# A graph network on one core: node features put in graph order by two scatters, indexed moves spaced out, and layer 0's edge weight as a polynomial on GpSimd

## The chip, the cores and the metric

The kernel runs on one core of one Trainium2 chip. A core has five engines that each work through their own list of instructions: TensorE (PE, with its weight loads shown apart as PEld), VectorE (DVE), ScalarE (ACT), GpSimd (POOL) and SyncE (SP), which here only issues DMAs. They meet at semaphores. The metric is the time of the program on the device in microseconds; lower is better.

## What is computed

There are 128 graphs of 64 nodes with 128 features each (`x`), and a 64x64 matrix `adj` for every graph, in which about a quarter of the entries are above zero (in a symmetric pattern). Four layers follow one another, each with a residual and a layernorm: `x = layernorm(x + layer(x, adj))`. The first two are message passings over the edges, and nearly all of the time is theirs:

```python
# layer 0: distance d = adj[i, j]
f_ij = jnp.exp(coeff * diff * diff)                 # 20 Gaussians of d
rcut = 0.5 * (jnp.cos(d_ij * (math.pi / CUTOFF)) + 1.0) * (d_ij < CUTOFF)
W = ssp(f_ij @ fw1 + fb1) @ fw2 + fb2               # ssp(x) = softplus(x) - log 2
agg = jnp.einsum('bjf,bijf->bif', y, W * rcut[..., None])   # y = x @ w_in2f
out = ssp(agg @ ow1 + ob1) @ ow2 + ob2
...
# layer 1: the same form with 64 Gaussians, and the entry of adj itself, twice, as the weight
```

Layers 2 and 3 are graph convolutions with a normalised `adj`. The part that the change touches is `rcut`, which depends on the distance alone: 0.5(cos(πd/5) + 1) is the square of cos(πd/10), and 0 from d = 5 on.

## The kernel before, in words

**Only edges that are there are computed.** The kernel (`sparse_stack`) sorts the graphs by their number of edges, and the nodes of each graph by their degree. Two graphs make a pair, so that their 2 x 64 nodes fill the 128 partitions. There are 64 pairs, in 8 sets `s` of 8 pairs (`part(s)`), and all pairs of a set have the same number of edge slots per node. `graph_to` (L891) is the new place of each graph; an indexed scatter (L892) writes all of `adj` in that order to the HBM scratch `adj_sorted`, from which `load_a` reads a set's matrices into `a_all`. The features are not sorted: `load_x(s)` (L1288) fetches each pair's 128 rows of `x` from the input by an indexed gather into `x_all[:, p, :]` (L1291), 8 per set, with the indices `at_row` that `find_rows` makes. Set 0 is different: its graphs are the first 16 as they stand, and a plain DMA loads them.

**Building the edge lists.** For a set `s`, `permuted(s)` (L1022) moves the rows of its matrices into the order of degrees: 8 indexed scatters of `a_all` rows to `perm` in HBM (helper `scatter`, L1017), then 16 SP loads back into the tile `ad` (L1057). `nearest(s)` (L1129) then finds each row's entries in descending order on DVE, eight at a time: MAX8 (L1155), FIND_INDEX8 (L1158), and two instructions that knock out what was found (L1163, L1167). `pack(0, s, ...)` (L1066) puts distances, indices and weights of the edges into slots: `dc` (distance minus 5, at least −5; the `tensor_scalar` with `max` at L1083) and `jc` (indices, L1097) on POOL, and the weight `w`, which is cos(πd/10) by a Sin on ACT, with a bias of π/2 (L1102), squared on POOL (DVE for set 0; L1104). The three go to HBM (`store`), and the main loop reads them back slot by slot (L1265). After `pack`, `edges` (DVE, L1175) counts what was found and writes to the first half of the tile `same`, which the search has used as its scratch; `equal` (POOL, L1178; DVE, L1183) uses the second half. At last `spread(s)` (L1194) sends the found rows by 8 indexed scatters to `rows1[s]`, from which layer 1's slots are packed.

**The function `act`.** All ACT work goes through `act` (L927). Exp, Ln, Square and Copy are in one table set, Sin is in another. `act` puts a table load ahead of each Sin and one after it (L935) and ties the order.

**The order of the work.** The main loop (L1874) has 128 slots (64 pairs for each of the two layers) of 3 chunks. A chunk is: `filter_in` (PE L1731, then Exp and Ln on ACT), `filter_out` (PE L1744), `gather` (PE L1757 with the one-hot matrix `hot`, then a copy on ACT), `message` (DVE L1772) and `slot_sums` (DVE L1796, L1800). `hot` is built once a slot on DVE from `j` and `w` (L1716). All other work is cut into steps by generators, and the loop takes some steps of each at every chunk: `run(early, ...)` takes 9, later 2 or 5, steps of `gathering`, which runs `compact(s)` for sets 1 to 7 one after the other; `run(side, 1)` takes one step of `spread`. Within `compact(s)`, `spread_out` (L1111) takes one step of the moves for the next set (`permuted(s + 1)`, then `load_x(s + 1)`) at every `PACE`-th (4th) step of the search, and what is left of them at the end. Set 0's edges are built before the loop. The order in which the steps are written out is the order on each engine: `in_order` fixes it for DVE and POOL before the loop and for all five engines inside it. So an instruction that has to wait holds up all that stands behind it on its engine. `edges`, for instance, stands on DVE ahead of the messages of later chunks.

Of the kernel before, what the change touches and what calls it, by code (L numbers as in the profile page):

```python
# [69 lines left out]
ROUNDS = (5, 4, 4, 4, 4, 3, 3, 3)  # L70
FAR = -1e30
X_LIMIT = 40.0


def offsets1():
# [526 lines left out]
def sparse_stack(ctx: ExitStack, tc: tile.TileContext, t: dict, out: bass.AP, flag):  # L602
# [59 lines left out]
    nc.vector.memset(ones, 1.0)  # L662
    neg_half = const.tile([P, NP], F32, name="neg_half")
    nc.gpsimd.memset(neg_half, -0.5)
    half_pi = const.tile([P, 1], F32, name="half_pi")
    nc.vector.memset(half_pi, PI / 2)
    half = const.tile([P, 1], F32, name="half")
    nc.vector.memset(half, 0.5)
    one = const.tile([P, 1], F32, name="one")
# [21 lines left out]
    a_all = const.tile([P, NP, A + 1], F32, name="a_all")  # L691

    adj_sorted = dram.tile([NB, A, A], F32, name="adj_sorted")
    x_all = const.tile([P, NP, C], F32, name="x_all")
    x_pairs = x.rearrange("(p b) n c -> (b n) p c", b=2)
    x_rows, out_rows = (v.rearrange("g n c -> (g n) c") for v in (x, out))

# [87 lines left out]
    def wait_steps(n):  # L785
        yield from (None for _ in range(n))
# [73 lines left out]
    with (  # L860
        tc.tile_pool(name="count", bufs=2) as pre,
        tc.tile_pool(name="count_ps", bufs=1, space=PSUM) as ps_pre,
    ):
        entries = pre.tile([NB, A, A], F32, name="entries", bufs=1)
        some = pre.tile([NB, A, A], BF16, name="some", bufs=1)
        within = pre.tile([NB, A, A], BF16, name="within", bufs=1)
        for q in range(4):
            cut = slice(16 * q, 16 * (q + 1))
            nc.sync.dma_start(entries[:, cut, :], adj[:, cut, :])
            nc.vector.tensor_scalar(within[:, cut, :], entries[:, cut, :], CUTOFF, None, ALU.is_lt)  # L870
            nc.vector.tensor_scalar(some[:, cut, :], entries[:, cut, :], 0.0, None, ALU.is_gt)


        degree, close = given[:, 0, :], given[:, 1, :]
        run(deque([count(some, pre, degree), count(within, pre, close)]), -1)
        nc.vector.scalar_tensor_tensor(close, close, -float(A), degree, ALU.add, ALU.add)

        total = const.tile([NB, 1], F32, name="total")
        nc.vector.tensor_reduce(total, given[:, 0:2, :], AX.XY, ALU.add)
        nc.vector.tensor_scalar(total, total, key_of[:, 0:1], key_of[:, 1:2], ALU.mult, ALU.add)  # L880
        keys = pre.tile([P, P], F32, name="keys", bufs=1)
        nc.vector.tensor_scalar(keys, ident, total, None, ALU.mult)
        keys_ps = ps_pre.tile([P, P], F32, name="keys_ps")
# [37 lines left out]

    fence, latest, kind = None, None, None

    def act(out_, in_, func, **kw):  # L927
        nonlocal fence, latest, kind
        now = func == AF.Sin
        if kind is None or now != kind:  # L930
            fence = latest
            if not now:
                ctx_ = tc.issue_after(fence.ins) if fence is not None else nullcontext()
                with ctx_:
                    fence = nc.scalar.preload_act_table_set("natural_log_exp_and_others")  # L935
            kind = now
        with tc.issue_after(fence.ins) if fence is not None else nullcontext():
            latest = nc.scalar.activation(out_, in_, func, **kw)  # L938
        return latest

# [125 lines left out]
    def pack(layer, s, d, j):  # L1066

        caps, bases = CAPS[layer][s], BASES[layer][s]
        even, odds = EVEN[layer][s], ODD[layer][s]

        def packed(name, dt):
            tile_ = cpt.tile([P, max(EVEN[layer])], dt, tag=f"{name}{layer}", name=f"{name}{layer}_{s}")
            return tile_[:, 0:even]

        dc, jc = packed("dc", F32), packed("jc", BF16)
        for r in range(8):
            to = slice(bases[r], bases[r] + caps[r])  # L1080
            engine = nc.vector if layer + s == 0 and r % 2 else nc.gpsimd
            if layer == 0:
                engine.tensor_scalar(dc[:, to], d[:, r, 0 : caps[r]], -CUTOFF, None, ALU.max)  # L1083
            else:
                engine.tensor_copy(dc[:, to], d[:, r, 0 : caps[r]])
            if r % 2:
                yield

        def store(name, tile_):
            for h, size in enumerate((even, odds)):  # L1090
                to = dram_ap(slots[layer, name][s], h * even, [[even + odds, 64], [1, size]])
                nc.sync.dma_start(to, tile_[64 * h : 64 * (h + 1), 0:size])

        store("d", dc)
        for r in range(8):
            to = slice(bases[r], bases[r] + caps[r])
            nc.gpsimd.tensor_copy(jc[:, to], j[:, r, 0 : caps[r]])  # L1097
        store("j", jc)
        w = packed("w", F32)
        if layer == 0:  # L1100
            yield from wait_steps(6 if s else 0)
            act(w, dc, AF.Sin, bias=half_pi, scale=PI / (2 * CUTOFF))  # L1102
            yield from wait_steps(PACE if s else 0)
            (nc.gpsimd if s else nc.vector).tensor_tensor(w, w, w, ALU.mult)  # L1104
        else:
            nc.gpsimd.tensor_tensor(w, dc, dc, ALU.mult)
        store("w", w)
        stored.add((layer, s))
        yield

    def spread_out(work, ahead, every):  # L1111

        for n, _ in enumerate(work):
            if n % every == 0:
                next(ahead, None)
            yield
        yield from ahead

    def compact(s):


        ahead = iter(())
        if 0 < s < NS - 1:
            ahead = chain(permuted(s + 1), load_x(s + 1))
        if 0 < s < NS - 2:
            load_a(s + 2)
        yield from spread_out(nearest(s), ahead, PACE)

    def nearest(s):  # L1129

# [20 lines left out]
        for k in range(max(ROUNDS)):  # L1151
# [9 lines left out]
            if more:  # L1161
# [4 lines left out]
                yield  # L1166
                nc.vector.scalar_tensor_tensor(now, gone[:, 0:more], FAR, now, ALU.mult, ALU.add)  # L1167
                yield
        yield from pack(0, s, top, at)


        edges, equal = (
# [21 lines left out]
    def spread(s, comb):  # L1194

        for r in range(8):
            scatter(
                rows1[s].rearrange("q a k -> q (a k)"),
                comb[:, r, :, :].rearrange("p a k -> p (a k)"), goes[s][:, r : r + 1],
            )  # L1200
            yield
        rows = big(f"rows{s}").rearrange("p (r a k) -> p r a k", r=8, a=2)
        nc.sync.dma_start(rows, rows1[s].rearrange("(q r) a k -> q r a k", r=8))
        yield
        yield
        yield from pack(1, s, rows[:, :, 0, :], rows[:, :, 1, :])
# [80 lines left out]

    def load_x(s):  # L1288

        for p in range(8 * s, 8 * (s + 1)):  # L1290
            nc.gpsimd.indirect_dma_start(  # L1291
                out=x_all[:, p, :], out_offset=None, in_=x_rows,
                in_offset=bass.IndirectOffsetOnAxis(ap=at_row[:, p : p + 1], axis=0),
            )
            yield

    load_a(0)
    nc.sync.dma_start(x_all[:, part(0), :], x_pairs[:, part(0), :])
# [138 lines left out]
    nc.tensor.matmul(u[:, 0:1], lhsT=w["w2"], rhs=h0, start=True, stop=True)  # L1437

    run(deque([node_before(0, 0)]), -1)
    run(deque([compact(0)]), -1)  # L1440
    zero_filter = const.tile([P, 1], F32, name="zero_filter")
    nc.vector.tensor_add(zero_filter, u[:, 0:1], w["b2"])
# [391 lines left out]
    slot_data[0] = loads(0, nc.scalar)  # L1834
    slot_data[1] = loads(1)
    run(deque([permuted(1)]), -1)
    side.append(load_x(1))
    nc.sync.dma_start(caps_dram, caps_row.rearrange("o s i r -> o (s i r)"))
    nc.sync.dma_start(
        caps.rearrange("g i r -> g (i r)"), dram_ap(caps_dram, 0, [[18, NS], [0, 16], [1, 18]])  # L1840
# [33 lines left out]
    for i in range(3 * N + 2):  # L1874
# [3 lines left out]

        run(sums, (1, 4, 4)[k])
        run(early, 9 if i < 18 else (PACE - 2, PACE + 1, PACE + 1)[k] if i < 3 * (NP - 8) else 7)  # L1880
        run(side, 1)
        run(stores, 1)
        if i == 3 * (NP + 5):
            assert not early and not side and not convs[0], "edges are still to be gathered"
# [101 lines left out]
```

## Time and profile before

| what | us |
|---|---|
| time, median of 3 runs (1686.64 to 1694.62) | 1686.74 |
| time of the profiled execution | 1728.7 |
| its span | 1726.9 |
| PE busy in the span | 1535.8 (89%) |
| DVE busy | 1511.8 (88%) |
| ACT busy | 1353.0 (78%) |
| POOL busy | 773.8 (45%) |
| the 56 gathers of `x` rows on POOL (L1291), together | 59.6 |
| the 8 table loads ahead of a Sin, together | 10.3 |

The times of the runs are taken without the profiler; the profiled execution is another one, and every duration in what follows comes from it. Its mean granted TensorE clock was 0.957 of full speed. A line of the profile names the line of the kernel, the engine, the operation, what it writes and reads ("out<-in"), how many there were, the busy time and the mean duration in ns, and then how long the engine had stood idle just before these instructions and what ended the idle time. A line of a table by stretches gives the stretch (us from the start of the span), its length, the busy time of PE, PEld, DVE, ACT and POOL with the number of instructions, the granted clock, the busy share of the DMA engines, and GB/s. A line of the timeline gives start, duration, engine, line, operation and, in brackets, the idle time ahead of it.

### The profile page before, as it was taken

To read this page: it belongs to the slowest core of one execution; us is meant where nothing else is said; L and a number is where in the kernel's file an instruction comes from. 1 tells how busy PE (TensorE), PEld (TensorE's weight loads), DVE (VectorE), ACT (ScalarE), POOL (GpSimd) and SP (SyncE) were. 2 spreads that over 40 slices of the span, in tenths; PEclk is the share of its full clock that TensorE was granted. 3 is DMA by queue.
4 is the path that set the end of the run, shared out by engine and by line. 5 is a ranking of instruction groups with operands and counts; after the bars stand their busy time and mean duration, and the time that the engine had idled before them with its cause. 6 is when DMAs were issued, how large, how long until landed. Compare 5 with 4: busy or idle time off the path is not lost. (4 is left out here: it accounts for less than half of the span.)

```text
span 1726.9 us, 24034 instructions
## 1 busy us (share of the span) xinstructions
PE 1535.8 (89%) x6813; PEld 792.4 (46%) x6813; DVE 1511.8 (88%) x4125; ACT 1353.0 (78%) x1699; POOL 773.8 (45%) x1173
## 2 busy tenths in 40 slices
PE   1367899999899999989999999999999999998975
PEld 1123344444444444445444555555555555544444
DVE  7668889999999888898888999999999899898885
ACT  1246688989888878879999988888888888888731
POOL 2446255655656534235112343444553354553334
PEclk9978899999999998999999999999999999999985
DMA  5354445554545443444766655555555445455200
GB/s 165 82 120 103 103 124 141 131 134 122 135 115 141 116 116 92 111 102 117 166 131 142 139 126 126 133 122 127 137 116 138 118 116 128 119 132 133 49 8 21
DMA packets 112656, 202.84 MB, mean 117 GB/s; under 512 B 47214, under 2 KB 63872, under 8 KB 112384
## 3 DMA queue, kind: packets, MB, share of 16 engines
q1 hardware_dynamic: 99856, 185.24, 44.8%
q0 software_dynamic: 8080, 14.47, 2.9%
q10 hardware_dynamic: 4576, 1.49, 0.4%
q8 instruction: 56, 0.92, 0.2%
q14 instruction: 88, 0.72, 0.1%
HBM read 186.66 MB, written 14.45 MB: 116 GB/s over the span
## 5 line engine op out<-in xcount | busy, mean ns | idle before, releaser
L938 ACT ACTIVATE g<-pg 128x672 f32<-128x672 f32 (+12 forms) x384 | 298.9, 778 | 159.0 <-PE pg L1757 120.0
L938 ACT ACTIVATE h<-h,half 128x672 f32<-128x672 f32 (+13 forms) x385 | 351.2, 912 | 12.5
L1757 PE MATMUL pg<-hot,ys 64*128 64x336 f32 (+12 forms) x1536 | 354.7, 539 | 4.6 <-issue 4.2
L1796 DVE TENSOR_REDUCE agg<-m 128x16 f32<-128x240 f32 (+13 forms) x896 | 325.0, 411 | 2.4
L1744 PE MATMUL pw<-h,w_L_gnn_fw 128*128 128x336 f32 (+6 forms) x768 | 281.5, 491 | 43.3 <-DVE m L1772 36.4
L1744 PE MATMUL pw<-h,w_L_gnn_W2T 128*128 128x420 f32 (+5 forms) x768 | 303.9, 519 | 3.3 <-DVE m L1772 3.2
L1772 DVE SCALAR_TENSOR_TENSOR m<-pw,c_L_gnn_fb,g 128x336 f32<-128x336 f32 (+6 forms) x384 | 202.0, 564 | 48.1 <-PE pw L1744 24.3
L1772 DVE SCALAR_TENSOR_TENSOR m<-pw,c_L_gnn_b,g 128x420 f32<-128x420 f32 (+5 forms) x384 | 226.3, 626 | 12.3 <-PE pw L1744 9.2
L938 ACT ACTIVATE h<-px,c_L_gnn_b 128x840 f32<-128x840 f32 (+5 forms) x192 | 176.8, 921 | 48.4 <-PE px L1731 46.3
L1731 PE MATMUL px<-d,fw 32*128 32x336 f32 (+6 forms) x768 | 169.9, 518 | 50.3 <-ACT d L938 28.0
L1757 PEld LDWEIGHTS pg<-hot,ys 64*128 64x128 f32 x1536 | 119.6, 191 | 187.8 <-ACT h L938 94.8
L1744 PEld LDWEIGHTS pw<-h,w_L_gnn_fw 128*128 128x128 f32 x768 | 138.3, 199 | 142.8 <-DVE m L1772 80.8
L1386 POOL TENSOR_TENSOR rs<-rs,neg_half 128x4 f32<-128x4 f32 x61 | 68.3, 1120 | 281.4 <-DVE rs L1383 280.0
L1744 PEld LDWEIGHTS pw<-h,w_L_gnn_W2T 128*128 128x128 f32 x768 | 133.1, 191 | 129.5 <-DVE m L1772 30.5
L1716 DVE SCALAR_TENSOR_TENSOR hot<-j,row,w 128x1212 f32<-128x1212 bf16 (+12 forms) x128 | 175.3, 1370 | 8.6 <-DMA w<-w_dram 8.6
L938 ACT ACTIVATE h<-px,c_L_gnn_fb 128x672 f32<-128x672 f32 (+6 forms) x192 | 158.4, 825 | 27.7 <-PE px L1731 9.5
L1731 PE MATMUL px<-d,w1t 64*128 64x420 f32 (+5 forms) x768 | 169.8, 519 | 0.0
L938 ACT ACTIVATE d<-d,neg_off 128x1212 f32<-128x1212 f32 (+12 forms) x128 | 136.3, 1065 | 5.2 <-DMA d<-d_dram 5.2
L1731 PEld LDWEIGHTS px<-d,fw 32*128 32x128 f32 x768 | 60.1, 190 | 147.6 <-issue 60.0
L1017 POOL DMA_INDIRECT rows<-comb,goes x64 | 70.7, 1104 | 113.4 <-DMA rows<-comb,goes 73.5
L1391 POOL TENSOR_SCALAR x_all<-ny,mv,rs 128x128 f32<-128x128 f32 x124 | 101.9, 828 | 3.4
L1017 POOL DMA_INDIRECT out_dram<-gz,at_row x56 | 73.8, 1318 | 52.7 <-DMA out_dram<-gz,at_row 41.2
(260 smaller groups left out, 2266.3 us busy)
## 6 DMA issues: line engine op xcount, KB each, us to landing
d<-d_dram SPq DMA_DIRECT2D x32, 315.0 KB
w<-w_dram SPq DMA_DIRECT2D x32, 315.0 KB
d<-d_dram SPq DMA_DIRECT2D x32, 303.0 KB
w<-w_dram SPq DMA_DIRECT2D x32, 303.0 KB
w<-w_dram SPq DMA_DIRECT2D x32, 252.0 KB
j<-j_dram SPq DMA_DIRECT2D x32, 157.5 KB
j<-j_dram SPq DMA_DIRECT2D x32, 151.5 KB
d<-d_dram SPq DMA_DIRECT2D x16, 300.0 KB
```

Of the source, the lines that this page charges most:

```text
L938: latest = nc.scalar.activation(out_, in_, func, **kw)
L1017: nc.gpsimd.indirect_dma_start(out=into, out_offset=bass.IndirectOffsetOnAxis(ap=at, axis=0), in_=rows, in_offset=None,)
L1386: nc.gpsimd.tensor_tensor(rstd, rstd, neg_half[:, 0:n], ALU.pow)
L1391: (nc.gpsimd if n == GS else nc.vector).tensor_scalar(dst[:, s, :], y[:, s, :], mv[:, s, 0:1], rstd[:, s : s + 1], ALU.subtract, ALU.mult,)
L1716: nc.vector.scalar_tensor_tensor(hots[n][:, 0:size], j[:, 0:size], near, wt[:, 0:size], ALU.is_equal, ALU.mult)
L1731: nc.tensor.matmul(ps[:, b, 0:n], lhsT=w["w1"][rows, :], rhs=d[rows, col : col + n], start=True, stop=True,)
L1744: nc.tensor.matmul(ps[:, 0 : c["size"]], lhsT=c["w"]["w2"], rhs=c["h"][:, b, :], start=True, stop=True)
L1757: nc.tensor.matmul(ps[:, b, 0:n], lhsT=y[rows, :], rhs=hots[c["n"]][rows, at], start=True, stop=True,)
L1772: nc.vector.scalar_tensor_tensor(messages[n][:, b, at], c["pw"][b][:, 0:size], c["w"]["b2"], c["g"][:, b, :], ALU.add, ALU.mult,)
L1796: nc.vector.tensor_reduce(av[:, :, :, r], both, AX.X, ALU.add)
```

## The change

It has three parts.

1. **Features in the order of graphs.** At the start, two plain loads bring all of `x` into SBUF, one row per graph: the first 48 nodes of each into the part of `x_all` that isn't used yet, the other 16 into the second half of `a_all`. After `node_before(0, 0)`, ahead of the first `compact`, two indexed scatters on POOL write them, graph by graph, to the HBM scratch `x_sorted` in the sorted order. `load_x(s)` is then four plain DMAs on SP in one step, in place of eight gathers on POOL in eight steps. `load_x(1)` runs before the loop, no longer in `side`.
2. **The other moves further apart.** `spread_out` takes a step of the moves at every 8th step of the search (`2 * PACE`); `spread` yields twice after each scatter, and the loop takes two steps of `side` if more than one generator is queued there, else one.
3. **The weight as a polynomial.** The Sin, its table loads and `half_pi` are gone. `cutoff` computes cos(πd/10) from t = dc + 5 by a polynomial of degree 4 in z = t², times t, and squares it. For sets 1 to 7 these are 12 POOL instructions on tiles of 128 partitions and 123 to 141 columns (6 `tensor_scalar`, 6 `tensor_tensor`); one of them, the last squaring, was there before. For set 0 DVE does it, with four `scalar_tensor_tensor` for the steps. t and z lie in the tile `same` (t at its start, z at column 320). The 10 empty steps that `pack` held between Sin, squaring and store are replaced by five.

```diff
+SINE = (7.76576612e-11, -5.98291300e-08, 2.55007753e-05, -5.16771008e-03, 3.14159264e-01)
...
+    x_flat = x.rearrange("g n c -> g (n c)")
+    parts = [x_all[:, 8 : NP - 8, :].rearrange("g i c -> g (i c)")]
+    parts.append(
+        a_all.rearrange("g p j -> g (p j)")[:, (A + 1) * NP // 2 :][:, 0 : A * C - parts[0].shape[1]]
+    )
+    x_parts = list(zip(parts, (slice(0, 48 * C), slice(48 * C, A * C))))
...
+        for into, at in x_parts:
+            nc.sync.dma_start(into, x_flat[:, at])
...
     def act(out_, in_, func, **kw):
-        nonlocal fence, latest, kind
-        now = func == AF.Sin
...
+        nonlocal fence
+        if fence is None:
+            fence = nc.scalar.preload_act_table_set("natural_log_exp_and_others")
+        with tc.issue_after(fence.ins):
+            return nc.scalar.activation(out_, in_, func, **kw)
...
+    def cutoff(w, dc, t, z, engine):
+        first, *others = SINE
+        def step(to, c, by):
+            if engine is nc.vector:
+                engine.scalar_tensor_tensor(to, to, c, by, ALU.add, ALU.mult)
+            else:
+                engine.tensor_scalar(to, to, c, None, ALU.add)
+                engine.tensor_tensor(to, to, by, ALU.mult)
+        engine.tensor_scalar(t, dc, CUTOFF, None, ALU.add)
+        engine.tensor_tensor(z, t, t, ALU.mult)
+        yield
+        engine.tensor_scalar(w, z, first, None, ALU.mult)
+        for n, c in enumerate(others):
+            step(w, c, z if n < len(others) - 1 else t)
+            yield
+        engine.tensor_tensor(w, w, w, ALU.mult)
...
         if layer == 0:
-            yield from wait_steps(6 if s else 0)
-            act(w, dc, AF.Sin, bias=half_pi, scale=PI / (2 * CUTOFF))
-            yield from wait_steps(PACE if s else 0)
-            (nc.gpsimd if s else nc.vector).tensor_tensor(w, w, w, ALU.mult)
+            t, z = (scratch[:, k * 320 : k * 320 + even] for k in range(2))
+            yield from cutoff(w, dc, t, z, nc.gpsimd if s else nc.vector)
...
-        yield from spread_out(nearest(s), ahead, PACE)
+        yield from spread_out(nearest(s), ahead, 2 * PACE)
...
-        yield from pack(0, s, top, at)
+        yield from pack(0, s, top, at, same)
...
                 comb[:, r, :, :].rearrange("p a k -> p (a k)"), goes[s][:, r : r + 1],
             )
             yield
+            yield
...
     def load_x(s):
-        for p in range(8 * s, 8 * (s + 1)):
-            nc.gpsimd.indirect_dma_start(
-                out=x_all[:, p, :], out_offset=None, in_=x_rows,
-                in_offset=bass.IndirectOffsetOnAxis(ap=at_row[:, p : p + 1], axis=0),
-            )
-            yield
+        for k, (first, last_) in enumerate(((0, 48), (48, A))):
+            from_ = x_sorted[k].rearrange("(p b) (n c) -> b n p c", b=2, c=C)
+            for b in range(2):
+                at = slice(b * A + first, b * A + last_)
+                nc.sync.dma_start(x_all[at, part(s), :], from_[b, :, part(s), :])
+        yield
...
     run(deque([node_before(0, 0)]), -1)
+    for into, (from_, _) in zip(x_sorted, x_parts):
+        scatter(into[:, :], from_, to)
...
-    side.append(load_x(1))
+    run(deque([load_x(1)]), -1)
...
-        run(side, 1)
+        run(side, min(2, len(side)))
```

More of the change, by code (lines that the diff above doesn't have):

```diff
@@ L664, in sparse_stack @@
     nc.gpsimd.memset(neg_half, -0.5)
-    half_pi = const.tile([P, 1], F32, name="half_pi")
-    nc.vector.memset(half_pi, PI / 2)
     half = const.tile([P, 1], F32, name="half")
@@ L693, in sparse_stack @@
     adj_sorted = dram.tile([NB, A, A], F32, name="adj_sorted")
+    x_sorted = [dram.tile([NB, n * C], F32, name=f"x_sorted{k}") for k, n in enumerate((48, 16))]
     x_all = const.tile([P, NP, C], F32, name="x_all")
     x_pairs = x.rearrange("(p b) n c -> (b n) p c", b=2)
-    x_rows, out_rows = (v.rearrange("g n c -> (g n) c") for v in (x, out))
+    out_rows = out.rearrange("g n c -> (g n) c")
+    x_flat = x.rearrange("g n c -> g (n c)")
[4 more added lines that the diff above has]
+    x_parts = list(zip(parts, (slice(0, 48 * C), slice(48 * C, A * C))))
     spare = x_all[:, NP - 8 :, :].rearrange("i p c -> i (p c)")
@@ L920, in dram_ap @@
         return bass.AP(tensor=ap.tensor, offset=ap.offset + offset, ap=dims)
-    fence, latest, kind = None, None, None
+    fence = None
     def act(out_, in_, func, **kw):
-        nonlocal fence, latest, kind
-        now = func == AF.Sin
[L930 to L939, printed above, removed]
+        nonlocal fence
[3 more added lines that the diff above has]
+            return nc.scalar.activation(out_, in_, func, **kw)
     codes = [const.tile([P, A], F32, name=f"code{i}") for i in range(2)]
@@ L1064, in goes_on, with pack @@
         nc.vector.tensor_scalar(goes[s], permuted_rows[s][:, :, A], row[:, 4:5], None, ALU.add)
-    def pack(layer, s, d, j):
+    def cutoff(w, dc, t, z, engine):
[14 more added lines that the diff above has]
+        engine.tensor_tensor(w, w, w, ALU.mult)
+    def pack(layer, s, d, j, scratch=None):
         caps, bases = CAPS[layer][s], BASES[layer][s]
```

## The prediction

> **What bounds the kernel now.** I read the page's busy table first, then busy time by stretch, then the timeline where VectorE (DVE) is idle, then the groups that the change touches. The profiled execution took 1728.7 us, of which the span is 1726.9; the median is 1686.74, so 42 us (2.5%) exist only under the profiler. I work the sum against 1728.7 and carry it to the median at the end.
>
> The page:
> ```profile
> PE 1535.8 (89%) x6813; PEld 792.4 (46%) x6813; DVE 1511.8 (88%) x4125; ACT 1353.0 (78%) x1699; POOL 773.8 (45%) x1173
> ```
> and stretches (us; busy PE, PEld, DVE, ACT, POOL with counts; TensorE clock; DMA share; GB/s):
> ```profile
> 100.00:120.00 20.00, 6.70 (x14) 2.31 (x16) 6.04 (x19) 4.03 (x5) 11.88 (x13) 0.53 0.48 111
> 160.00:180.00 20.00, 8.07 (x31) 4.48 (x30) 7.07 (x30) 3.12 (x4) 13.26 (x14) 0.66 0.36 87
> 240.00:260.00 20.00, 18.80 (x86) 8.88 (x84) 19.83 (x69) 17.84 (x23) 9.77 (x23) 1.00 0.46 116
> 320.00:340.00 20.00, 18.67 (x88) 9.26 (x87) 19.30 (x61) 18.50 (x26) 11.63 (x10) 1.00 0.47 116
> 1000.00:1100.00 100.00, 99.75 (x465) 53.16 (x465) 93.82 (x218) 88.19 (x103) 48.51 (x50) 1.00 0.59 133
> ```
> Layer 0's messages run from about 80 to 760 us; there DVE is full (19.83 of 20), since it finds the neighbours of later sets beside its own work. Layer 1 belongs to PE (99.75 of 100), and the change takes nothing from PE. So only layer 0 can gain, and only where DVE stands still. It does so in two holes: 20 − 6.04 and 20 − 7.07, together 26.9 us. POOL alone is busy in them:
> ```profile
> 104.41 0.98 POOL L1291 DMA_INDIRECT x_all<-in_x_dram,at_row  x1 [0.30 <-issue]
> ...
> 110.74 0.77 ACT L938 ACTIVATE g<-pg 128x720 f32<-128x720 f32 x1 [8.75 <-remote]
> ...
> 112.10 0.94 POOL L1291 DMA_INDIRECT x_all<-in_x_dram,at_row  x1 [0.30 <-issue]
> ...
> 118.58 1.09 DVE L1772 SCALAR_TENSOR_TENSOR m<-pw,c_L_gnn_fb,g 128x360 f32<-128x360 f32 x2 [10.10 <-remote]
> ```
> Nine x gathers run back to back while ACT, PE and DVE stand without a releaser in the kernel. The second hole coincides with the next set's gathers and moves. I read both as bursts of indexed moves that hold up whatever else needs the DMAs; the trace shows the coincidence, not the cause. Groups, with busy us, mean ns, idle before:
> ```profile
> L1291 POOL DMA_INDIRECT x_all<-in_x_dram,at_row x56 | 59.6, 1064 | 25.8 <-issue 14.2 <-DVE g L1428 11.1 <-DVE at L1158 0.3
> L938 ACT ACT_TABLE_LOAD x8 | 10.3, 1283 | 17.4 <-DVE dc L1083 17.3
> L938 ACT ACTIVATE w<-dc,half_pi 128x130 f32<-128x130 f32 (+6 forms) x8 | 3.2, 405 | 0.1
> L1104 POOL TENSOR_TENSOR w<-w 128x130 f32<-128x130 f32 (+5 forms) x7 | 3.5, 496 | 26.0 <-ACT w L938 25.9
> ```
>
> **What the Trainium skill says.** *ScalarE: Activation LUTs*, "What ACT_TABLE_LOAD costs": about 1283 ns plus a drain for each switch of table set. The trace agrees (1283 above); a Sin stands between two loads and keeps ACT from 645.52 to 648.52, 3.0 us. *GPSIMD Engine Reference*, "3.1 Elementwise — side-by-side cycle accounting": a two-input tensor_tensor is about half as fast as on VectorE. The trace gives 402 ns for 128x130 on POOL, and no equal shape on DVE. *SBUF — State Buffer*, "Who interferes with whom": a two-input VectorE instruction and a GpSimd one that reads SBUF exclude each other for a whole instruction. This fits one of the seven squarings, which took 1057 ns at 128x141 beside 402 for 128x130, and a DVE `goes` of 1.43 us beside POOL work against 0.38 to 0.44 elsewhere. *DMA: Bandwidth & Descriptors*, "Issuing engines are not separate DMA queues": every transfer goes through the same 16 DMA engines. That supports reading the holes as contention.
>
> **The change, part by part.**
>
> *Gathers and moves.* 56 gathers leave POOL, 59.6 us, which costs nothing by itself: POOL is 45% busy. What can be won is the 26.9 us of holes: without the gathers, and with moves every 8th step in place of every 4th, no burst like 104–115 is left. The 8 `perm` moves and their 16 `ad` loads of a set stay, so a part of a hole may stay: ends 0 and −27, in the profile −27. If the holes go, DVE's own work is next, so no more than they hold is won. Whether an execution without the profiler has them is open: it is 42 us shorter, and layer 1, full of PE work, has no such time to give. I take half, −13, for the median.
>
> *The new loads.* Two SP loads (4 MB) and two scatters (4 MB) at the start. `entries`, 2 MB, took 10.5 us (0.7 to 11.2), and the adjacency scatter, 2 MB, 5 us (28.75 to 33.75). The scatters issue from about 45 us, beside the first compaction on DVE (47.9 to 66), which no DMA feeds: their 10 us (4 MB at that pace) are hidden; without that cover they cost 10. The loads land about 20 us later than `entries`, at about 31, ahead of the first adjacency part on SP's queue and of ACT's waits on shared DMA lanes; ACT's `rows` copy begins at 37.0. The `j` and `d` stores of set 0 (63.8 us) stand behind load_x(1), which waits for the scatters, done at about 58. I take +1; ends −0.5 and +6. Afterwards each set puts 4 loads on SP, 4 × 0.6 = 2.4 us (the 0.6 is a `w` load's issue), past the slot loads; SP itself waits there for buffers (378.9 us in 80 waits on `hot`), so 0; without that slack, 7 × 2.4 = 17.
>
> *Moves further apart.* A set had 17 steps at every 4th (68 yields); it has 10 at every 8th (80), the leftover running at the end one by one. Nothing waits sooner: 0; were the last `ad` loads late, 7 sets × 1 us, an estimate.
>
> *Sin out of ACT.* Seven Sins lie in the loop (set 0's lies ahead of it; there 4 DVE steps replace two loads and a Sin, 0). DVE busy in the 10 us around each:
> ```profile
> 138.20:148.20 10.00, 7.53 (x34) 3.24 (x32) 9.65 (x26) 9.68 (x12) 5.46 (x9) 1.00 0.58 143
> ...
> 559.30:569.30 10.00, 7.59 (x32) 4.06 (x28) 6.21 (x15) 9.79 (x13) 4.97 (x8) 0.83 0.47 115
> 644.50:654.50 10.00, 7.16 (x24) 3.13 (x22) 4.75 (x15) 9.57 (x13) 2.02 (x7) 0.82 0.45 118
> sum 70.00, PE 56.36 PEld 26.65 DVE 52.88 ACT 67.76 POOL 41.04; mean PE 8.05 PEld 3.81 DVE 7.55 ACT 9.68 POOL 5.86
> ```
> 70 − 52.88 = 17.1 idle, with ACT full (67.76 of 70). Quiet stretches idle 0.2 to 0.7 in 20 us, about 2 for these 70. So 15 at most; ends −4 (if half follows from PE and the set's end, and part of the rest is queued again) and −15; I take −10.
>
> *The polynomial on POOL.* Per set 12 instructions in place of one. Six tensor_tensors at 0.40. Six tensor_scalars: POOL's `dc` takes 0.244 at 14 columns and 0.307 at 30, the two-operation one on 128 columns 0.797; bounds 0.35 and 0.80, taken 0.6. With some 0.1 between (an estimate; `dc` shows 0.07): 6 × 0.4 + 6 × 0.6 + 11 × 0.1 = 7.1 us. POOL has the time. But the scratch is the tile `same`, which DVE's `edges` (L1175) then overwrites: DVE now waits for the polynomial's 11th instruction. Behind it on DVE are the messages (L1772) and `hot` (L1716), for which PE and ACT wait. By the order of the changed kernel's instructions, set 1 has only two messages' worth (about 2 us) between the last search and `edges`: wait ≈ 6.6 − 2 = +4.6. Sets 2 to 7 have about 11 us there (`hot` 1.3, messages and sums 9), which hides 6.6 plus one POOL task of 1.3: 0. Added exclusion with DVE's two-input work: 77 more POOL instructions, minus 56 gathers that go; taken +5, ends 0 and +11 (77 × 0.14). Sum +10; ends +3 and +30, the latter with every instruction at 1.06: eleven are a chain of 12.7, set 1 then +10.7, six sets +1.7 and 1.5 for a task between.
>
> **Sum.** Profile: −27 + 1 − 10 + 10 = −26, or 1702.7. Median: −13 + 1 − 10 + 10 = −12, or 1675.
>
> **Rivals.**
> (a) *The holes are there without the profiler too and close wholly*: −26, 1661; with full Sin gain and a cheap polynomial 1650. For: ACT, PE and DVE stop together for 7 to 10 us while POOL works. Against: 42 us of the profiled run do not recur.
> (b) *The holes are the profiler's, or the moves that stay keep them*: 0 + 1 − 10 + 10 = +1, 1688. For: the second hole holds moves and `ad` loads too (15.3 us for the 16 instead of 6.2).
> (c) *DVE's wait at `edges` becomes the bound*: POOL's chain behind indexed moves, each instruction near 1.06, passes the 11 us window: 10.7 + 6 × 3.2 = 30, exclusion within it; with the holes half closed −13 + 1 − 10 + 30 = +8, 1695; with them left +21, 1708. About 1702. It decides from the point where the chain with what is queued in it exceeds 11 us. For: 1057 ns was seen once in seven. Against: the other six average 0.40.
> (d) *The x detour is late at the start*, +6 more on (b): 1693, no change by the bound below.
>
> **How the numbers follow.** Forecast 0.42 (1667 to 1683), (a) 0.25 (1650 to 1667), (b) with (d) 0.20 (1683 to 1694), (c) 0.13 (1695 to 1710). 0.5% of the time, 8.4 us, is about what a measurement of this kernel tells from no change: faster is below 1678.3, slower above 1695.2. Faster: 0.25 and 0.36 of the forecast's 0.42, 0.61; same: 0.06 + 0.20 + 0.01 = 0.27; slower 0.12. The range leaves out a little of (a) and half of (c): 1654 to 1700.
>
> **What would show it.** Right: no 20 us stretch of layer 0 with DVE under 12; no table load in the loop; `edges` waiting on POOL about 5 us once, under 1 in the other sets; POOL's added tensor_scalars near 0.6. Wrong: holes that stay at the `perm` moves; waits at `edges` in most sets; `rows` or the first messages later than 37 and 80.8 us; PE short of full in layer 1.

## The result and the profile after

The changed kernel is slower: 1718.53 us (median of 4 runs, 1710.46 to 1723.52) against 1690.68 us (1686.64 to 1698.11) for the kernel before on the same occasion; ratio 1.0136, 95% interval 1.0106 to 1.0166. The forecast was 1675, range 1654 to 1700.

Its profiled execution took 1713.9 us (span 1712.1). The page's first line, and the stretches that were shown of before:

```profile
PE 1535.9 (90%) x6813; PEld 795.8 (46%) x6813; DVE 1518.3 (89%) x4131; ACT 1330.8 (78%) x1675; POOL 766.1 (45%) x1196
```
```profile
100.00:120.00 20.00, 15.25 (x56) 5.98 (x56) 19.86 (x86) 13.58 (x17) 2.11 (x9) 0.91 0.50 111
160.00:180.00 20.00, 18.44 (x84) 8.59 (x84) 19.68 (x71) 17.41 (x24) 2.64 (x4) 1.00 0.53 123
240.00:260.00 20.00, 20.00 (x84) 9.57 (x84) 18.76 (x67) 15.66 (x20) 11.84 (x23) 0.93 0.38 99
1000.00:1100.00 100.00, 99.76 (x463) 52.50 (x459) 93.83 (x215) 87.45 (x101) 45.72 (x47) 1.00 0.55 128
```

The two holes are gone (DVE 19.86 and 19.68 where it had 6.04 and 7.07), and layer 1 is as it was. The groups of the polynomial on POOL, and the DVE instruction that now waits behind it (busy us, mean ns, idle before):

```profile
L1079 POOL TENSOR_SCALAR w<-w 128x130 f32<-128x130 f32 (+5 forms) x28 | 15.5, 554 | 2.4
L1080 POOL TENSOR_TENSOR w<-w,same 128x130 f32<-128x130 f32 (+5 forms) x28 | 13.0, 465 | 2.3
L1085 POOL TENSOR_SCALAR w<-same 128x130 f32<-128x130 f32 (+5 forms) x7 | 5.3, 762 | 0.2
L1197 DVE TENSOR_SCALAR_CACHE_REDUCE same<-comb 128x320 f32<-128x320 f32 x8 | 3.8, 479 | 12.3 <-POOL w L1080 12.2
```

The timeline at set 1, where `edges` (now L1197) stands still until the 11th of POOL's 12 instructions is done:

```profile
127.35 0.58 POOL L1079 TENSOR_SCALAR w<-w 128x141 f32<-128x141 f32 x1
128.01 0.48 POOL L1080 TENSOR_TENSOR w<-w,same 128x141 f32<-128x141 f32 x1
128.52 0.49 DVE L1197 TENSOR_SCALAR_CACHE_REDUCE same<-comb 128x320 f32<-128x320 f32 x1 [4.38 <-POOL w L1080]
```

So single prices and the wait of set 1 (4.4 us, forecast 4.6) came out as worked, though sets 2 and 5 wait too (3.6 and 4.2 us); the holes went, and yet the time rose. Two things have to be explained: where the gain went, and what costs some 25 us.

A reader needs one fact for the numbers below: the kernel before takes near 1692 us on some occasions and near 1725 us on others, for reasons outside the kernel (the five later occasions were on five chips, so that the chip and the time cannot be told apart), and each ratio is against runs of the kernel before on the same occasion.

### The profile page after: what moved, and what is told of

The parts are those of the page before. It is cut to its first block, busy times and chain, and to the rows that moved or that the text cites. A ratio compares the mean times of both kernels' runs of the same rounds, so it can differ in the third digit from the quotient of the medians.

```text
span 1712.1 us, 24073 instructions
## 1 busy us (share of the span) xinstructions
PE 1535.9 (90%) x6813; PEld 795.8 (46%) x6813; DVE 1518.3 (89%) x4131; ACT 1330.8 (78%) x1675; POOL 766.1 (45%) x1196
## 4 chain that ended last, share of the span: by engine, by line
PE 38%; DVE 23%; issue 12%; POOL 11%; DMA 10%; ACT 4%; SPq 1%; ACTq 0%; DVEq 0%; POOLq 0%
PE pw L1769 13%; PE pg L1782 8%; PE px L1756 7%; DMA out_dram<-gz,at_row 6%; DVE m L1797 5%; POOL x_all L1414 4%; DVE agg L1821 4%; ACT h L942 2%; POOL rs L1409 2%; DVE hot L1741 2%; DVE at L1180 2%; POOL gz L1414 2%; PE y L1439 1%; DMA w<-w_dram 1%; PE o L1571 1%
## 5 line engine op out<-in xcount | busy, mean ns | idle before, releaser
L1414 POOL TENSOR_SCALAR x_all<-ny,mv,rs 128x128 f32<-128x128 f32 x124 | 106.9, 869 | 3.3
```

The source lines that it names most:

```text
L1414: (nc.gpsimd if n == GS else nc.vector).tensor_scalar(dst[:, s, :], y[:, s, :], mv[:, s, 0:1], rstd[:, s : s + 1], ALU.subtract, ALU.mult,)
```

## The experiments

Five theories stand in the expectations. A: the loss is DVE's wait behind the polynomial. B: it is the loads and scatters of `x` and the later moves. C: POOL's added work costs by itself. D: spacing the moves costs, through late second moves of sets 0 and 1. E: the empty steps that left `pack` with the Sin matter, since they set how fast the search runs against the loop. In e0_before_again (below), in e4 and in e9 the letters A and B stand for the narrower claims that those texts spell out.

| run | what it is | before, us | this, us | ratio (95%) |
|---|---|---|---|---|
| result | all three parts | 1690.7 | 1718.5 | 1.0136 (1.0106 to 1.0166) |
| e4 | all three parts | 1693.1 | 1724.8 | 1.0151 (1.0099 to 1.0203) |
| e5 | all, polynomial behind the counting | 1693.1 | 1729.8 | 1.0230 (1.0197 to 1.0264) |
| e6 | all, polynomial on DVE | 1693.1 | 1717.9 | 1.0145 (1.0110 to 1.0179) |
| e7 | part 1 alone | 1693.1 | 1695.0 | 1.0012 (0.9989 to 1.0035) |
| e16 | all, 5 empty steps at a set's end | 1693.3 | 1695.3 | 1.0011 (0.9985 to 1.0036) |
| e17 | all, 5 empty steps ahead of `edges` | 1693.3 | 1692.1 | 0.9978 (0.9958 to 0.9997) |
| e1 | parts 1 and 2 | 1725.8 | 1714.4 | 0.9924 (0.9895 to 0.9954) |
| e2 | part 3 alone | 1725.8 | 1758.2 | 1.0157 (1.0109 to 1.0206) |
| e3 | all, t in a tile of its own | 1725.8 | 1734.5 | 1.0039 (1.0013 to 1.0064) |
| e9 | part 2 alone | 1724.0 | 1734.4 | 1.0080 (1.0054 to 1.0106) |
| e10 | parts 1 and 3 | 1724.0 | 1725.7 | 1.0006 (0.9986 to 1.0026) |
| e11 | part 1, polynomial spread | 1724.0 | 1718.9 | 0.9963 (0.9938 to 0.9989) |
| e13 | part 1 alone | 1725.4 | 1703.6 | 0.9869 (0.9839 to 0.9898) |
| e14 | all three parts | 1725.4 | 1734.4 | 1.0055 (1.0039 to 1.0071) |
| e15 | part 1, polynomial spread, empty steps kept | 1725.4 | 1701.4 | 0.9852 (0.9812 to 0.9892) |

### Are the holes in the kernel before, and whose are they?

The kernel before was profiled three times more, without an edit.

> The kernel before, unchanged, for a second profile. Theory A (the polynomial costs: the two holes of DVE at 100 to 120 and 160 to 180 us belong to that one profiled execution, 1728.7 us, and are no part of a usual one near 1690): span near 1688 to 1700, and no 20 us stretch of layer 0 with DVE under 12 us. Theory B (the holes are in every execution, and the loss is in what the change adds for x): DVE again near 6 to 7 of 20 in both stretches, or in others as long.

> The kernel before, a third profile. Where its time on this chip is near 1690, the trace should have no stretch of layer 0 with DVE idle for 5 us or more with releaser remote or issue, and layer 0 near 722 us; where it is near 1726, the holes at slots 1 and 5 are there again and layer 0 is near 757. If a run near 1690 has the holes, they are the profiler's after all.

> The kernel before, a fourth profile. The three so far (1728.7, 1739.6, 1725.3 us) all have the holes of DVE at slots 1 and 5. If this run is near 1690, it should have none over 5 us there, and layer 0 near 722 us, as part 1 alone had; if it is near 1725, the holes again, and layer 0 near 755.

They took 1739.6, 1725.3 and 1736.0 us, all on occasions near 1725, and all have the holes. The stretches of the last one, under them those of part 1 alone on the same occasion (e13), and then those of part 2 alone (e9), which keeps the gathers but takes them at every 8th step of the search:

```profile
100.00:120.00 20.00, 4.30 (x10) 1.59 (x12) 5.01 (x17) 1.94 (x3) 11.80 (x13) 0.56 0.40 100
160.00:180.00 20.00, 8.23 (x28) 3.23 (x28) 8.73 (x39) 3.90 (x5) 14.79 (x16) 0.68 0.34 90
```
```profile
100.00:120.00 20.00, 16.42 (x64) 7.12 (x62) 17.83 (x75) 14.67 (x19) 2.44 (x3) 1.00 0.35 90
160.00:180.00 20.00, 15.64 (x55) 7.51 (x55) 13.60 (x44) 14.46 (x20) 0.73 (x1) 0.75 0.57 117
```
```profile
100.00:120.00 20.00, 13.60 (x44) 5.45 (x44) 14.58 (x64) 12.66 (x16) 3.98 (x4) 0.74 0.33 79
160.00:180.00 20.00, 17.31 (x49) 8.08 (x50) 14.24 (x41) 12.91 (x17) 3.86 (x4) 0.66 0.37 85
```

Part 1 alone is e7 and e13: the changed kernel with the Sin and the old pace,

```diff
-        yield from spread_out(nearest(s), ahead, 2 * PACE)
+        yield from spread_out(nearest(s), ahead, PACE)
...
-        run(side, min(2, len(side)))
+        run(side, 1)
```
and with `act` and the Sin as before.

> Part 1 alone: features in graph order by two scatters and plain loads, the Sin on ACT and the pace of the moves as before. If the gathers' bursts make the holes, this has the whole gain of parts 1 and 2: 0.989 to 0.996, no wait of DVE over 5 us with releaser remote or issue. If the spacing of the moves does it, 0.998 to 1.004, and the holes stay where perm moves run every 4th step.

> Part 1 alone again. If the gathers' bursts make the holes, and an occasion with before near 1725 has them: ratio 0.982 to 0.988 on such an occasion (26 us), since the sum of the other runs there says so: parts 1 and 2 took 13 us off, part 2 alone put 14 us on. On an occasion with before near 1690: 0.998 to 1.004 as before. If part 1 takes nothing even where before shows 1725, the holes have another cause.

Where before is near 1725, part 1 is worth 1.3% (22 us of medians), about the 27 us of the holes. Where before is near 1693, it is worth nothing. So most of the holes goes with the gathers. A part stays without them: in e13, 15 moves to `perm` and `perm_again` follow one another on POOL from 140 to 161 us, ACT stands 8.6 us without a releaser in the kernel up to 162.8, and DVE is busy for 13.6 of the 20 us of the second stretch. And in e9 the holes are a third to a half as deep though the gathers are still there. This fits bursts of indexed moves of any kind, gathers above all. The occasions near 1692 are, as far as the times tell, those without the holes; no trace of the kernel before on such an occasion was had, so that half is inferred. The result was measured on one of them: the gain was not there to be had.

### What costs: the parts

Parts 1 and 2 with the Sin kept (e1), part 3 alone (e2), part 2 alone (e9), parts 1 and 3 (e10), and the changed kernel again:

> Parts 1 and 2 of the change alone: features in graph order and moves further apart, with the Sin on ACT as before. Theory A (the loss comes from the polynomial on GpSimd, where DVE's edges instruction waits for it, 12.2 us in three waits in the trace after, and from what follows it): no slower than before, ratio 0.994 to 1.002. Theory B (the loss comes from the x loads, scatters and the later moves: hot waits 9.0 us for the ad loads, goes 5.3 us for a DMA): slower by 10 to 28 us, ratio 1.006 to 1.017.

> Part 3 alone: the polynomial in place of the Sin, with the gathers of x and the pace of the moves as before. Theory A: most of the 28 us is here, ratio 1.007 to 1.017, with waits of DVE's edges on POOL of 12 us or more in sum. Theory B: near 1.000, 0.996 to 1.004.

> Part 2 alone: moves at every 8th step and spread twice as far apart, with the gathers and the Sin as before. Theory D (part 2 makes the second moving of set 0 and 1 late, so that goes waits for the ad loads, 4.7 to 6 us at slot 30 in the changed kernel, with the slots 28 to 35 longer by some 11 us): slower by 5 to 12 us, ratio 1.003 to 1.008 on a chip where before is near 1690. Theory A (part 2 is free, the goes wait comes from the polynomial's instructions ahead of the moves on POOL): 0.997 to 1.003. On a chip where before has the holes, some 10 us less in either case.

> Parts 1 and 3: features in graph order and the polynomial on POOL, with the pace of the moves as before. Theory A (part 3 makes the loss): 12 to 16 us of waits at edges and equal, less some 6 us that the Sin had cost, plus late moves, ratio to before 1.010 to 1.016 on a chip with before near 1690. Theory D (part 2 is half of it): 1.003 to 1.008.

> The changed kernel, unchanged, beside the other kernels of this call on one chip. Theory A (the two holes of DVE, some 27 us, are in an execution of the kernel before only on some chips or occasions, and the changed kernel never has them): the ratio to before depends on whether before shows near 1690 or near 1726 here: about 1.014 in the first case and 1.000 to 1.010 in the second. Theory B (the holes are the same everywhere): 1.011 to 1.017 again.

> The changed kernel a third time. With before near 1725: if the costs of parts 2 and 3 add up (14 and 27 us) to the gain of part 1 (26), 1.007 to 1.010; if parts 2 and 3 overlap as they seem to where before is near 1690 (25 us together), 0.997 to 1.002. With before near 1690: 1.011 to 1.017.

Part 3 costs 1.6% alone; theory B falls with e1 and e13. On top of part 1 it costs 1.0006 against 0.9869, some 1.4%. Part 2 on top of part 1 costs 0.9924 against 0.9869 (e1 and e13), and on top of parts 1 and 3 1.0055 against 1.0006 (e14 and e10): twice some 0.5%, 9 us, where before is near 1725. Part 2 alone costs 0.8% (10 us of medians), which was forecast at 0, and is more than D had for an occasion near 1725; its trace still has DVE standing for remote and issue, 18.3 us in its two largest such groups. With 17 steps of moves per set taken at every 8th of 89 steps of the search, some five are left over and run at the set's end, so that a set takes longer; the search starts 7.8 slots apart, in place of 7.3. In the changed kernel, with 10 steps of moves, none is left, and neither in e1, so this does not explain the 0.5%, whose cause stays open.

### Is it the wait at edges?

In e3 t has a tile of its own, so `edges` is free of the polynomial:

```diff
-            t, z = (scratch[:, k * 320 : k * 320 + even] for k in range(2))
+            t = cpt.tile([P, max(EVEN[0])], F32, tag="poly_t", name=f"poly_t{s}")[:, 0:even]
+            z = scratch[:, 320 : 320 + even]
```

> The changed kernel with t of the polynomial in a tile of its own, so that DVE's edges need not wait for the polynomial; z stays at column 320 of the search's scratch tile. Theory A: the 12 us of waits go, a part comes back one step later, where DVE's second equal instruction waits for POOL's subtraction behind the polynomial: 8 to 15 us faster than the changed kernel, ratio to before 1.004 to 1.011. Theory B: as the changed kernel, 1.011 to 1.017.

1.0039 against 1.0055 for the changed kernel on another such occasion: little. The wait had moved one step on, to `equal` behind POOL's subtraction, 14.8 us in place of 12.8 at `edges`:

```profile
DVE same L1206 <- POOL same L1201: 14.8, 4, 6.1
```

In e5 the polynomial runs behind the counting, after the product that ends it:

> The changed kernel with the polynomial of sets 1 to 7 moved behind POOL's part of the edge counting (the subtraction, the copy and the product), so that neither edges nor the second equal on DVE stands behind it. Theory A (the loss is DVE's wait behind the polynomial's instructions on POOL, at edges, or one step later at equal when edges is freed): no such wait over 2 us, and the time at or below that of parts 1 and 2 alone, ratio 0.983 to 0.994. Theory C (POOL's added time costs by itself: exclusion with DVE, or the perm_again and rows moves late behind it): as with t in a tile of its own, 1.000 to 1.007.

Slower still, and against A's number. What is late now is the next set's memset on POOL, behind which the next set's first MAX8 waits:

```profile
DVE comb L1179 <- POOL comb L1165: 32.8, 6, 10.0
```

So moving the chain as a block only moves the wait. In e6 it is on DVE (one word: `nc.vector` for every set), and no wait at all is left behind it:

> The changed kernel with the polynomial on DVE for all sets, 8 instructions per set of about 0.25 us each, 2 us per set, 14 us in the seven sets, straight into the engine that is full. Theory A: no waits at edges, but all 14 us are paid: 0.996 to 1.003, slower than the version with the polynomial later on POOL. Theory C: POOL's time is what costs, so this is the fastest of the call, 0.985 to 0.996.

As slow as the changed kernel, 1.0145. The polynomial's DVE work is 22.4 us in eight sets, 2.8 us each where 2 were expected, and stands in place of the waits; that could still be read as A with one price for another. All three kernels have the changed kernel's 84 steps per set. The next runs change the steps.

### The empty steps

e11 is part 1 with the polynomial as two POOL instructions at each chunk, from a queue of its own and in tiles of its own:

```diff
+            if s > 0:
+                polys.append(later(s, w, dc, even, store))
+                return
...
         run(side, 1)
+        run(polys, 1)
```
and e15 is the same with `yield from wait_steps(11)` ahead of that `return`.

> Part 1, and the polynomial on POOL in tiles of its own, one step (two instructions) at each chunk of the loop, so that nothing of edges, equal, the next memset or the moves stands behind the whole chain. Theory A (queueing behind 12 instructions in a row is the cost): the Sin's 6 us are won and nothing is paid, ratio 0.993 to 0.999 where before is near 1690, 0.985 to 0.995 where it is near 1726. Theory C (POOL's 50 us of added work cost DVE by themselves): 1.003 or more.

> Part 1, the polynomial spread over chunks on POOL, and 11 empty steps left in pack where the Sin's waits were, so that the search stands at the same slots as before (edges of set 7 near slot 46, not 40). Theory E (part 3 also loses by taking out empty steps: the search crowds into fewer slots, and late steps meet DMAs that have not landed, 7.5 us at slot 42): no such wait, and the Sin's gain is left: ratio to before 0.993 to 0.999 with before near 1690, 0.977 to 0.985 near 1725. Theory C (POOL's added work by itself): as slow as the version without the empty steps, 1.003 or more and 0.994 to 0.999.

The two differ in empty steps alone, and by 1.1% (0.9963 against 0.9852, on two occasions near 1725). A's price, a chain in a row, is absent in both. C falls too: with the steps kept, POOL's added work costs nothing that is seen (e15 0.9852, e13 0.9869). Then the changed kernel itself, with five empty steps per set put back, e16 at the end of a set, e17 ahead of `edges`:

```diff
+            yield from wait_steps(5)
...
+            yield from wait_steps(5 if s else 0)
```

> The changed kernel with 5 empty steps put back per set, behind the product that ends the edge counting, so that a set takes as many steps as before; the distance from the search to edges stays short. Theory E (some 16 us of part 3's cost are the missing steps, which crowd the search into earlier slots and let late steps meet DMAs that have not landed): about 10 to 16 us faster than the changed kernel: ratio to before 0.996 to 1.000 where before is near 1725, 1.004 to 1.008 where it is near 1690; the waits at edges (12 to 13 us) stay. If the waits at edges are all that matters: no gain, 1.004 to 1.008 and 1.012 to 1.017.

> The changed kernel with the same 5 empty steps per set put between the polynomial and its store, ahead of edges, so that DVE has more of the loop's work before it comes to edges. If both count: the waits at edges fall under 4 us and the search stands where it stood before; 8 to 16 us faster than with the steps at the end, 0.986 to 0.994 where before is near 1725, 0.994 to 1.002 where it is near 1690. If the wait at edges is free because something else is late then: as with the steps at the end.

e16 takes away all of the loss: 1.0011 against 1.0136 and 1.0151, 21 to 24 us, by steps in which nothing is done. (The three ratios are from three occasions, with before at 1693.3, 1690.7 and 1693.1; near 1725 neither e16 nor e17 was run, and there e11 and e15 stand for the steps.) The waits at `edges` did not go. Waits (us, times, longest) of e4, e16 and e17, a fence each:

```profile
DVE m L1797 <- PE pw L1769: 34.2, 41, 3.3
...
DVE same L1197 <- POOL w L1080: 12.8, 3, 5.0
```
```profile
DVE m L1798 <- PE pw L1770: 18.1, 28, 2.2
...
DVE same L1197 <- POOL w L1080: 11.8, 2, 6.8
```
```profile
DVE m L1798 <- PE pw L1770: 26.5, 35, 4.5
...
DVE same L1198 <- POOL w L1080: 3.9, 2, 2.7
```

In e16 the 11.8 us at `edges` are paid, and DVE stands 16 us less for PE. e17 takes 8 us of that wait away too, and the time falls by 3 us (medians 1695.28 and 1692.07, 5 us by the means; the intervals of the ratios just meet, and in the two profiles as much comes back as waits for PE, 26.5 in place of 18.1). So at this pace A explains 3 to 5 us, not 25. Against the kernel before of its own occasion, e17 is a little faster where before is near 1692 (0.9978, its interval just clear of 1), and e15 is 1.5% faster where before is near 1725. Each beats both the kernel before and the changed one there.

How do empty steps act? The loop takes 12 steps of the compaction in a slot (2, 5 and 5 at its three chunks). A set has 89 steps before (1 for the start, 68 of the search, 15 in `pack`, 5 in the counting), 84 in the changed kernel, 78 in e11. The slot, in thirds for its chunks, at which the search of sets 2 to 7 starts in DVE's order, counted by the messages ahead of it in the traces of e7, e4, e16, e11 and e9, and the mean distance from set 3 on:

```
part 1 alone      4.3 10.3 17.7 25.0 32.3 39.7    89 steps: 7.3 slots apart
changed           4.3  9.3 16.3 23.3 30.3 37.3    84 steps: 7.0
steps at the end  4.3 10.3 17.7 25.0 32.3 39.7    89 steps: 7.3
spread, no steps  4.0  8.3 14.7 21.3 27.7 34.3    78 steps: 6.5
part 2 alone      4.7 11.0 18.7 26.7 34.7 42.3    94 steps: 7.8
```

With fewer steps DVE has the same search to do in fewer slots. It ends earlier, but the slots after it get nothing back: from the `hot` of slot 44 to that of slot 64 it is 211.5 us in e4, 211.0 in e16 and 215.7 in e7. From the `hot` of slot 0 to that of slot 44 it is 546.0, 514.2 and 509.0 us, and of the 32 us that e4 needs beyond e16, 24 are idle time of DVE. Besides crowding, DVE waits 7.5 us in e11 for weights that the step behind the last set loads (`w<-in_L_gnn_fw_dram`), a wait that e15 and e16 do not have.

The clock is the last piece. Three stretches of layer 0 (82 to 300, 300 to 500, 500 to 690 us) in e4, then in e16; the granted clock is the third column from the end:

```profile
82.00:300.00 218.00, 189.02 (x735) 86.10 (x731) 194.49 (x654) 158.04 (x201) 116.74 (x192) 0.91 0.52 126
300.00:500.00 200.00, 178.93 (x777) 88.45 (x776) 179.34 (x591) 158.27 (x209) 112.99 (x191) 0.94 0.50 123
500.00:690.00 190.00, 176.61 (x764) 89.28 (x762) 166.20 (x502) 150.52 (x204) 84.64 (x165) 0.91 0.45 113
```
```profile
82.00:300.00 218.00, 192.89 (x802) 90.18 (x801) 200.89 (x683) 171.28 (x217) 115.92 (x189) 0.95 0.54 131
300.00:500.00 200.00, 181.58 (x807) 90.06 (x806) 186.25 (x598) 163.69 (x220) 116.53 (x201) 0.95 0.52 128
500.00:690.00 190.00, 179.22 (x816) 89.59 (x816) 176.19 (x537) 160.90 (x218) 94.05 (x163) 0.97 0.47 120
```

In the same number of us e4 gets fewer matmuls done, at a lower clock. The Trainium skill, *TensorE: Matmul & The Clock Gate*, "What's actually happening", says that the clock is halved after an idle window of some 3.4 us. The traces show half clock after windows that are far from idle. Two places of e4, each with 3.4 us at full clock and the half clock behind it:

```profile
127.23:130.64 3.41, 0.85 (x6) 0.42 (x4) 0.96 (x3) 2.98 (x4) 3.04 (x6) 1.00 0.74 129
130.64:140.88 10.24, 8.38 (x16) 3.36 (x16) 10.07 (x35) 2.53 (x3) 8.97 (x11) 0.50 0.76 175
```
```profile
485.60:489.00 3.40, 2.10 (x10) 0.90 (x10) 3.30 (x15) 3.33 (x5) 2.62 (x4) 1.00 0.70 199
489.01:492.42 3.41, 3.41 (x10) 1.31 (x10) 3.38 (x17) 0.14 (x2) 3.24 (x5) 0.50 0.16 43
```

The first is the stop at `edges` of set 1, with PE busy for 0.85 of 3.41 us; before the second PE was busy for 2.10. In the clock records all changes lie on one grid of 3.41 us. Over layer 0 of all 20 profiles, each of the 162 windows of this grid at full clock in which PE was busy for less than 1.7 us was followed by half clock, none of the 3332 with more than 2.4 us was, and of the 281 between them 112 were. So here it is enough that PE is busy for less than half of such a window, as the profile models its matmuls.

Summed over layer 0, the clock records show half clock for 106 us in e4, 89 in the profile after, 61 in e16, 58 in e17 and 55 in e7. Over 20 profiles of all these kernels, clock time lost (half of that) and length of layer 0 go together, with a correlation of 0.91. A wait that leaves PE short of work is thus followed by half clock in these traces, and so by a second cost, DVE waiting for a slow PE. The 34.2 against 18.1 us of e4 and e16 fit this; the 26.5 of e17, whose clock is as good as e16's, fit less well. No run changed the clock alone, so this is an association, not a cause shown.

What is shown is that the five steps cost; how they do so, down to the chunk, stays open. Fewer steps are not worse by a general rule: e9, with 94, loses too. And 84 steps are just seven slots, so that in the changed kernel every set from set 3 on starts at the same chunk of its slot (the table above), which it does not with 89. e16 and e17 change this together with the pace, and no run parts the two; e11, which loses as well, has no such fixed place.

## Why the prediction was wrong, by its own steps

**"42 us exist only under the profiler" fell.** The 1713.93 of the profile after is itself one of the timed runs, so what stands ahead of the change, that the times are taken without the profiler, does not hold for every run. For the edited kernels the profiled execution lies between 5 us below and 9 us above its median, and the later profiles of before (1725 to 1740) stand 1 to 14 us above medians near 1725. So the 42 us were, as far as the runs tell, mainly the difference of two occasions.

**"I take half, −13, for the median" was no size that ever occurs.** Part 1 with its loads measured +2 us (e7, within its interval of nothing) on an occasion like that of the result, and −22 (e13) on the other. The mechanism (gathers in a burst stop the engines) fits e13 and e9; a part of it stays with the moves to `perm`, as rival (b) had it.

**"The new loads": +1.** Right in the profile of the result: the first copy of g stands at 81.3 us after, 80.8 before. In other profiles of kernels with part 1 it stands at up to 87.8 us (e13 85.1, e17 86.5, e15 87.8), so the end of +6 occurs too; e15 and e17 are the fastest of their occasions all the same.

**"Moves further apart … Nothing waits sooner: 0" was wrong alone** (e9, +0.8%), for a reason the prediction counted and dropped: leftover steps "at the end one by one" lengthen a set. With part 1 the leftover is nil; there part 2 measured +9 us near 1725 (e1 against e13), and near 1693 it is no more than the noise (e16 and e17, with parts 2 and 3, against e7). The second moves of set 0 still come late: `goes` waits 4.1 us in e16.

**Sin out, −10, and polynomial, +10.** POOL's 6 tensor_scalars measured 0.55 to 0.76 us (taken 0.6), its tensor_tensors 0.40 to 0.51 (taken 0.40), a chain of some 7 us. The +5 for exclusion rested on 0.14 us per instruction, which the prediction works out from no line, and nothing of it is seen: e15, with the polynomial on POOL, is as fast as e13. The reading behind it is right for the squaring of 1057 ns, which starts inside a `hot` with two inputs in SBUF; the `goes` of 1.43 us has one input of 8 columns, and the eight of them took 0.21 to 1.43 us, not 0.38 to 0.44. The wait came in three sets, 12.2 us, where one at 4.6 was forecast: sets 2 and 5 were said to be hidden. Yet e16 against e17 prices most of it at 3 to 5 us. With the steps kept, Sin out and polynomial in together come to −3 to 0 us (e15 against e13, e16 and e17 against e7): the sum of 0 was right.

**The step that failed is one that the sum lacks.** The prediction used the yields of a set to see that the moves end in time, and never asked what five fewer of them do to the pace. That term measured +21 to +24 us (changed against e16). With it the sum reads, where before is near 1692: +2 for part 1, about 0 for Sin, polynomial and pace of the moves, +22 for the steps, together 24; the result was 23 by its ratio. (The +22 is the difference between the changed kernel and e16, so this shows what is left for the other terms, and is no second proof.) The rival on the slower side, (c), named DVE's wait at `edges` and about 1702 us. It had the direction, but the result was 1718.53, above its range of 1695 to 1710, and the wait was 3 to 5 us of it: that it had the direction is luck.

## What to carry to other kernels

Where a hand-written loop deals out background work by steps, empty steps are part of the schedule: an edit that takes some out changes the rate of everything behind it, and has to be compared at equal pace before its own cost is judged. A wait that leaves TensorE short of work may cost more than its length if the granted clock falls after it, which here took less than a full stop; compare the clock by stretch, not only the waits. And a stall seen in one profiled execution is a gain only where the timed runs have it: compare the profile's own time with the median, and look at a second profile before crediting it.

## What was not expected of the hardware

The kernel before differs by 2% (1692 and 1725 us) from occasion to occasion, each on another chip, and a kernel that avoids bursts of indexed gathers differs less: part 1 alone 1695.0 and 1703.6. The clock was halved after windows of 3.41 us in which PE was busy for up to 2.1 us (e4), and after every one under 1.7. A wait of DVE can be long and cost less than it lasts: 11.8 us at `edges` in e16 against 3.9 in e17, for 3 to 5 us of time. On POOL the same `tensor_scalar` shape took 0.55 us on average within the chain, 0.59 as its first instruction and 0.76 as the first that writes `w`.
